# Two transformer layers on one core: the whole first-layer feed-forward is put ahead of the attention loop, and the second layer's weight transform goes one product to a gap

## The chip, the cores and the metric

The kernel runs on one core of a Trainium2 chip. The metric is device time in microseconds (us), the median of several runs. One execution was also recorded by the hardware profiler; all views of the profile below are of that one.

## The reference, cut to what matters

The input is 2 batches of 1024 tokens, 256 wide. Each of two layers normalises the tokens and adds an attention branch and a feed-forward branch, both computed from the same normalised tokens:

```
x = x + linear_attention(xn) + ffn0(xn)      # first layer, xn = layernorm(x)
x = x + softmax_attention(xn) + ffn1(xn)     # second layer, 16 heads of 16, rotary q and k
ffn0: silu(xn @ wu.T) * (xn @ wg.T) @ wd.T   # weights made ternary, 1024 hidden
ffn1: the same shape; its input and its hidden layer each go through a
      Walsh-Hadamard transform and a sign vector (SU_ug, SU_dp)
```

The kernel never transforms the tokens of ffn1. It transforms the three weight matrices once instead. A transform over 256 is a product with a 128x128 Hadamard matrix in each of two halves, and then the sum and the difference of the halves. So the effective up and gate weights are `su * (H @ w[half 0] + H @ w[half 1])` and `su * (H @ w[half 0] - H @ w[half 1])`. The down weights are handled alike over 1024, with three levels of sums and differences ("butterflies") behind the products.

## The kernel before, in words

**Two stretches.** The first layer, the second layer's attention heads of the first half of the heads of batch 0, and the search for the score maxima of the first unit stand in a prologue that a planner orders. The second layer's softmax attention is a loop written out by hand, and it takes everything else in as filler.

**The planner** (`Plan`, lines 158 to 269) records the prologue's operations in groups ("norm 1", "piece 3", "search 2" and so on), gives each a cost (`cost`, line 341), and sets them in an order by list scheduling: the operation that can begin first goes first, and between several on one engine the longest remaining chain wins. `LEADS` (line 48) holds four numbers for each group, one an engine, that are added to that chain. They do no work; they only move groups against each other. `BURST` is the planned cost of one search step.

**First-layer feed-forward.** The 2048 tokens are eight pieces of 256 columns. A piece (`ffn0`, line 750) is 8 hidden blocks of 128: 8 TensorE products each into the PSUM tile `pug` (4 for up, 4 for gate, since the tokens are split into a high and a low fp32r half `xs`), then ScalarE's tanh, two VectorE products (or, with `by_pool`, one VectorE product, a ScalarE `gate` copy and a GpSimd product), and the split of the result into `hid` high and low by ScalarE and GpSimd. Then 32 down products into `py`, and two additions to `x`. Pieces 0 to 3 are recorded wide (two blocks at a time), pieces 4 and 5 (`AHEAD = 2`, line 47) with `by_pool`, and pieces 6 and 7 (`piece0`, line 829) are filler of the loop.

**The search** (`search`, line 1294) finds the score maxima of the first unit: 32 steps, each one tile `sc` of two PSUM banks, 4 products of 32 rows (two heads by high and low), and one VectorE reduction of 128x1024 into `peak`. The step's two heads lie on two of the four 32-row groups of the array; step j+1 has the other two. There are two such two-bank tiles ("pair").

**The loop** (line 1463) has 8 units (batch, group of 4 heads). Units 0 to 6 have 32 slots each. A slot begins with a burst of 10 products on all four row groups: the scores of the next unit into `scm` (for the maxima, reduced by VectorE into `peak`) and the scores of this unit into `sce` (ScalarE's exponential into `pr`). Behind each burst comes a gap, which holds, every other iteration, 8 products with the values (`po`), the heads of the next half (`pqkv`, `pt`) in units 0, 2 and 4, and filler. `fill` (line 1339) spreads the filler by planned cost: what is left over the slots that are left. `go_on` and the marks SOON, FIRST, SECOND, BOTH decide at which point of a slot a generator goes on. Unit 7 has no `scm`; its 16 bursts are 12 products of `sce`.

**The filler in order**: pieces 6 and 7, the weight transform (`hadamards`, line 1050), the norms of the second batch, and the eight pieces of ffn1 (`ffn`, line 524: 32 fp32 products into `pug` and 16 into `py` each).

**The weight transform before.** `load_raw` (line 963) fetches six raw halves of 512 KB on SyncE's queue into a ring of three tiles that the norms and splits share. `hadamard_in` (line 976) does two products `pw` of 128x512 in one gap, and makes the sum and the difference out of PSUM: per half two ScalarE `eff` products and two VectorE `eff` operations. `hadamard_down` does the same with the down weights, one VectorE product each, and the butterflies run beside it on VectorE, GpSimd and ScalarE.

All recorded operations pass through one line of the file (316), so groups are told apart by their tiles.

Of the kernel before, what the change touches and what calls it, by code (L numbers as in the profile page):

```python
# [46 lines left out]
AHEAD = 2  # L47
LEADS = {
    "norm 0a": (-475, -452, -511, -447),
    "norm 0b": (-470, -454, -445, -428),  # L50
    "norm 1": (206, -498, -315, -178),
    "project 0": (-283, -287, -271, -286),
    "project 1": (-379, -378, -411, -385),
    "state 0": (-460, -471, -464, -465),
    "attend 0": (-328, -267, -237, -351),
    "attend 1": (-359, -315, -855, -567),
    "wuT0": (162, -329, -317, -571),
    "wgT0": (-376, -396, -368, -395),
    "wdT0": (-512, -476, -556, -527),
    "piece 0": (-333, -279, -282, -449),  # L60
    "piece 1": (-242, -206, -275, -311),
    "piece 2": (-363, -220, -404, -211),
    "piece 3": (-515, -540, -507, -534),
    "norm1 0": (-316, -213, -275, -243),
    "heads 0": (-257, -293, -242, -251),
    "norm1 1": (-308, -257, -154, -234),
    "heads 1": (-323, -80, -413, -578),
    "search 0": (-842, -831, -846, -843),
    "search 1": (-260, -228, -261, -275),
    "search 2": (-273, -536, -274, -367),  # L70
    "search 3": (-1183, -1191, -1182, -1171),
    "norm 2": (-418, -435, -436, -416),
    "norm 3": (-414, -434, -376, -387),
    "project 2": (-625, -621, -635, -600),
    "project 3": (-821, -804, -840, -810),
    "state 1": (-1258, -1149, -1268, -1233),
    "attend 2": (-298, -223, -266, -308),
    "attend 3": (-351, -334, -344, -324),
    "piece 4": (-302, -105, -189, -341),
    "piece 5": (-325, -374, -399, -449),  # L80
}
FREE = ("stats", "mv", "rstd", "shift", "rz", "part")
BURST = 0.65
# [275 lines left out]
def tile_two_layers(ctx: ExitStack, tc: tile.TileContext, a: dict, out: bass.AP):  # L359
# [469 lines left out]
    def piece0(cc):  # L829

        yield from ffn0(cc, load_raw if cc == 7 else lambda: split0(cc + 1))

# [116 lines left out]
    su_ug = load(const, "su_ug", a["su_ug"], [P, 2])  # L949
# [8 lines left out]


    raws = [("wdT1", 0), ("wdT1", 1), ("wgT1", 0), ("wgT1", 1), ("wuT1", 0), ("wuT1", 1)]  # L960
    loaded = []

    def load_raw(count=2):
        for _ in range(count):
            if raws:
                name, n = raws.pop(0)
                raw = at.tile([P, 2, C], F32, tag="stage", name="raw", bufs=3)
                if name == "wdT1":
                    view = a[name].rearrange("(k p) n -> p k n", p=P)[:, 4 * n : 4 * n + 4, :]
                    sync.dma_start(out=raw.rearrange("p a (b n) -> p (a b) n", b=2), in_=view)  # L970
                else:
                    view = a[name].rearrange("(k p) n -> p k n", p=P)[:, :, n * C : (n + 1) * C]
                    sync.dma_start(out=raw, in_=view)
                loaded.append(raw)

    def hadamard_in(name, tag):

        eff = const.tile([P, 2, E], F32, tag=tag, name=f"eff_{name}")
        had[name] = eff
        for n in range(E // C):  # L980
            cols = slice(n * C, (n + 1) * C)
            raw = loaded.pop(0)
            pw = []
            for k in range(2):
                pw.append(bank("pw"))
                mm(pw[k], [(hm, raw[:, k, :])])
                if k == 0:
                    yield C * COL
            load_raw(1)
            yield C * COL, SOON  # L990
            for m in range(2):
                scalar.mul(eff[:, m, cols], pw[1], su_ug[:, m : m + 1])
                op = ALU.subtract if m else ALU.add
                vector.scalar_tensor_tensor(eff[:, m, cols], pw[0], su_ug[:, m : m + 1], eff[:, m, cols], ALU.mult, op)
            for t in pw:
                shut(t)
            yield 0.0

    def hadamard_down():
        wd1 = const.tile([P, NB, D], F32, tag="wC", name="wd1")  # L1000
        had["wdT1"] = wd1
        there = []
        for n in range(2):
            raw = loaded.pop(0)
            for i in range(2):
                pw = bank("pw")
                mm(pw, [(hm, raw[:, i, :])])
                if i:
                    load_raw(1)
                yield C * COL, SOON  # L1010
                e = 4 * n + 2 * i
                vector.tensor_mul(
                    wd1[:, e : e + 2, :], pw.rearrange("p (k n) -> p k n", k=2), ws_dp.unsqueeze(1).to_broadcast([P, 2, D])
                )
                shut(pw)
                yield 0.0
            there.append(4 * n)
            if n == 0:
                background.append(butterflies(wd1, there))
# [29 lines left out]

    def hadamards():  # L1050
        yield from hadamard_down()
        yield from hadamard_in("wgT1", "wA")
        yield from hadamard_in("wuT1", "wB")
# [240 lines left out]
    def search(part):  # L1294

        for i in range(STEPS // 4):
            j = part // 2 * 16 + part % 2 * 2 + i // 2 * 4 + i % 2
            sc = pair("sc")
            plan.burst = True
            burst(scores_of(0, j, sc))  # L1300
            plan.burst = False
            scores_max(0, j, sc)
            yield
# [35 lines left out]
    def fill(us, queue, k=0, alone=False):  # L1339


        spent[k] = begun = max(spent[k], -1.0) - us
        while spent[k] < 0 and queue:
            when = waits.get(queue[0], 0)
            if ordered[0] and when == SOON and alone and spent[k] - begun < LEAD:
                spent[k] = min(spent[k], -LEAD)
            elif ordered[0] and (when in (FIRST, SECOND) or (when == SOON and spent[k] > -LEAD)):
                break
            step(queue, k)
        if not queue:  # L1350
            spent[k] = max(spent[k], 0.0)

    def go_on(*when):

        if filler and waits.get(filler[0], 0) in when:
            step(filler)
# [24 lines left out]
    ffn0_cost = 8 * NB * F * PASS + 2 * D * NB * 2 * PASS  # L1381
# [44 lines left out]
    for cc in range(4, 4 + AHEAD):  # L1426
# [7 lines left out]
    split0(4 + AHEAD)  # L1434
# [3 lines left out]
    layer0 = [piece0(cc) for cc in range(4 + AHEAD, 8)]  # L1438
    filler += [*layer0, hadamards(), lambda: norm1(2), lambda: norm1(3)]
    filler += [ffn1(cc) for cc in range(8)]  # L1440
    left[0] = (4 - AHEAD) * ffn0_cost + 2 * norm_cost + 12 * C * COL + 8 * ffn1_cost + 3 * heads_cost + attention_cost
# [7 lines left out]
    def slot(weight, heads=True):  # L1449
# [6 lines left out]
        fill(max(share - heads, 0.0), filler, alone=heads == 0.0)  # L1456
# [6 lines left out]
    for u in range(len(units) - 1):  # L1463
        if u in (0, 2, 4):

            if u:
                while any(g in filler for g in layer0):
                    step(filler)
# [56 lines left out]
def _layout(i):  # L1525


    def cols(v):
        return v.reshape(-1, P).T

    def halves(kind):
# [18 lines left out]
        "su_ug": cols(i["L1_ffn_SU_ug"]),  # L1550
# [23 lines left out]
```

## Time and profile before

| | us |
|---|---|
| median of 3 runs (878.51 to 878.73) | 878.65 |
| the profiled execution, device time | 879.28 |
| its span, first to last instruction | 877.5 |
| prologue, to the first `scm` product | 204.0 |
| units 0 and 1 of the loop | 89.4 and 97.4 |
| units 2 to 6, each | 83.8 to 86.2 |
| unit 7 with the end | 59.7 |

The profiled execution is 0.63 us above the median. A unit's length is the distance of its first burst from the next unit's, read off the timeline. One first-layer piece's GpSimd and ScalarE work can be read from the list of groups: `act` 750 ns and `hid` 751 ns on GpSimd, `gate` 472 ns on ScalarE, each of 128x256. In the list of groups an fp32 product shows as two records and an fp32r product as one. TensorE's durations there overlap, since products are pipelined, so this text takes distances from start to start where it wants a price.

### The profile page before, as it was taken

The numbers are of one execution on the slowest core, as the hardware profiler recorded it, in microseconds if no ns is written. First come the engines' busy times: TensorE is split into PE (matmuls) and PEld (weight loads), VectorE is DVE, ScalarE is ACT, GpSimd is POOL, SyncE is SP. The second block draws the span as 40 slices with busy tenths as digits, with TensorE's granted clock in tenths as the row PEclk, the third lists the DMA queues.
The fourth block names the chain that finished last, engine by engine and source line by source line (L and its number), as shares of the span: only waits on it lengthen the run. The fifth ranks groups of instructions, "written<-read, shape, count | busy, mean of one in ns | idle before, by whom it ended". The sixth has DMA issues, their size and how long they took to land.

```text
span 877.5 us, 14602 instructions
## 1 busy us (share of the span) xinstructions
PE 848.7 (97%) x6048; PEld 507.7 (58%) x6048; DVE 578.5 (66%) x957; ACT 446.1 (51%) x660; POOL 211.1 (24%) x285
## 2 busy tenths in 40 slices
PE   8999999999999989899999999999999999999997
PEld 5699866675556535455555555555555555555543
DVE  5887575876877778557866656577675766666311
ACT  6646465514666466345554544455454544444654
POOL 2656867522552133004400000054000000000000
PEclk9999999999999999999999999999999999999999
DMA  9200000000000200000000000000000000000001
GB/s 304 90 1 1 1 1 1 1 25 1 1 26 1 70 27 1 1 1 1 1 1 1 1 1 1 1 1 19 31 1 1 1 1 1 1 1 2 1 5 44
DMA packets 11313, 14.77 MB, mean 17 GB/s; under 512 B 1264, under 2 KB 8944, under 8 KB 11248
## 3 DMA queue, kind: packets, MB, share of 16 engines
q1 hardware_dynamic: 11248, 13.85, 4.7%
q8 instruction: 47, 0.77, 0.3%
q14 instruction: 18, 0.15, 0.1%
HBM read 11.75 MB, written 2.10 MB: 16 GB/s over the span
## 4 chain that ended last, share of the span: by engine, by line
PE 83%; DVE 10%; ACT 4%; issue 2%; DMA 1%; POOL 0%; SPq 0%; ACTq 0%; DVEq 0%; POOLq 0%
PE pug L316 18%; PE scm L316 16%; PE py L316 14%; PE po L316 13%; PE sce L316 8%; PE pqkv L316 5%; DVE peak L316 4%; PE pt L316 4%; PE pkv L316 2%; ACT pr L316 1%; PE sc L316 1%; PE pq L316 1%; DVE act L316 1%; PE pw L316 1%; DVE t_wgT L316 1%
## 5 line engine op out<-in xcount | busy, mean ns | idle before, releaser
L316 ACT ACTIVATE pr<-sce 128x1024 f32<-128x1024 f32 x256 | 260.5, 1024 | 268.6 <-PE sce L316 268.5
L316 DVE TENSOR_REDUCE peak<-scm 128x2 f32<-128x1024 f32 x224 | 274.0, 1223 | 159.9 <-PE scm L316 157.6
L316 PE MATMUL po<-pr,va 128*17 128x512 f32 x1024 | 124.9, 596 | 0.0
L316 PE MATMUL sce<-qk_hi 32*128 32x512 f32 x512 | 122.4, 496 | 2.0 <-DVE peak L316 1.1
L316 PE MATMUL scm<-qk_hi 32*128 32x512 f32 x448 | 112.1, 496 | 2.9 <-DVE peak L316 2.2
L316 PEld LDWEIGHTS scm<-qk_hi 32*128 32x128 f32 x448 | 41.5, 182 | 111.6 <-DVE peak L316 42.0
L316 PE MATMUL sce<-mx,ones_r 32*128 32x512 f32 x512 | 97.0, 392 | 0.1
L316 PE MATMUL sce<-ql,qk_hi 32*128 32x512 f32 x512 | 96.9, 393 | 0.0
L316 POOL CAST tops<-nm 128x16 fp32r<-128x16 f32 x16 | 3.6, 226 | 372.6 <-DVE nm L316 367.6
L316 PE MATMUL scm<-qk_hi,ql 32*128 32x512 f32 x448 | 89.3, 394 | 0.0
L316 PE MATMUL pug<-xnT,eff_wuT 128*128 128x256 f32 x256 | 72.4, 392 | 0.0
L316 PE MATMUL pug<-xnT,eff_wgT 128*128 128x256 f32 x256 | 69.8, 395 | 0.9 <-DVE hid L316 0.9
L316 PE MATMUL py<-wd,hid 128*128 128x256 f32 x256 | 67.1, 398 | 1.8 <-DVE xnT L316 1.8
L316 DVE SCALAR_TENSOR_TENSOR act<-act,pug 128x256 f32<-128x256 f32 (+1 forms) x112 | 50.5, 452 | 25.7 <-ACT act L316 21.0
L316 PEld LDWEIGHTS po<-pr,va 128*17 128x17 f32 x1024 | 22.8, 96 | 63.0 <-issue 61.3
L316 PEld LDWEIGHTS py<-wd,hid 128*128 128x128 f32 x256 | 45.5, 190 | 23.2 <-issue 18.7
L316 POOL TENSOR_TENSOR hid<-act,hid 128x256 fp32r<-128x256 f32 (+1 forms) x48 | 44.4, 930 | 51.6 <-ACT hid L316 39.9
L316 PEld LDWEIGHTS pug<-xnT,eff_wgT 128*128 128x128 f32 x256 | 45.0, 189 | 18.9 <-issue 13.2
L316 PEld LDWEIGHTS pug<-xnT,eff_wuT 128*128 128x128 f32 x256 | 45.6, 189 | 15.4 <-issue 10.7
L316 DVE TENSOR_TENSOR x<-py,x 128x256 f32<-128x256 f32 x68 | 27.8, 418 | 39.0 <-PE py L316 38.5
L316 PEld LDWEIGHTS sce<-mx,ones_r 32*128 32x128 f32 x512 | 46.4, 183 | 11.0 <-ACT mx L316 0.5
L316 PEld LDWEIGHTS sce<-qk_hi 32*128 32x128 f32 x512 | 45.8, 182 | 10.4 <-ACT pr L316 4.9
(146 smaller groups left out, 1338.3 us busy)
## 6 DMA issues: line engine op xcount, KB each, us to landing
out<-x SPq DMA_DIRECT2D x16, 128.0 KB, 1.7
x<-in_x SPq DMA_DIRECT2D x3, 512.0 KB, 9.4
both<-in_wuT SPq DMA_DIRECT2D x1, 1024.0 KB, 9.5
both<-in_wgT SPq DMA_DIRECT2D x1, 1024.0 KB, 10.7
wdT<-in_wdT SPq DMA_DIRECT2D x1, 1024.0 KB, 13.2
raw<-in_wdT SPq DMA_DIRECT2D x2, 512.0 KB, 3.6
raw<-in_wgT SPq DMA_DIRECT2D x2, 512.0 KB, 3.3
raw<-in_wuT SPq DMA_DIRECT2D x2, 512.0 KB, 3.4
```

The costliest lines, as they stand in the source:

```text
L316: return call(*map(real, args), **{k: real(v) for k, v in kw.items()})
```

## The change

- All of pieces 4 to 7 are recorded in the planner's prologue with `by_pool` (`AHEAD` and `piece0` go).
- A search step pair is one burst: 8 products on all four row groups into two tiles, then two reductions. `BURST` is 0.70 for the two, where it was 0.65 for one. `LEADS` has new numbers for all groups.
- `load_raw` issues three whole loads of 1 MB at the loop's start, into the tiles that held the ternary weights of the first layer (`wA`, `wB`, `wC`). In the program SyncE issues gate, up, down in this order.
- The sums and differences of the halves are made on the raw weights, ahead of the products, by GpSimd (`sums_in`): 4 differences into `less` and 4 sums in place, 128x512 each. The sign vector goes into the Hadamard matrix once (`hm_su`, two small VectorE products).
- `hadamard_in` and `hadamard_down` do one product in a gap and then move on to the next gap; the PSUM result is copied out by ScalarE or VectorE in turn, with no arithmetic. Two slots of `pause` stand ahead.
- `fill` is left out where the slot's share is used up, and a generator marked BOTH as filler goes on at any of the slot's points but LAST.

Counted in the two programs, TensorE's products are the same 4882. VectorE has 18 instructions fewer, ScalarE 12 more and GpSimd 24 more.

In the changed program unit 0's gaps hold the heads and the twelve `pw` products, each in a gap of its own or beside heads; ffn1 begins two slots before unit 1.

```diff
-AHEAD = 2
 LEADS = {
-    "norm 0a": (-475, -452, -511, -447),
+    "norm 0a": (-1158, -1159, -1192, -1189),
...
+    "piece 6": (-1028, -1111, -943, -903),
+    "piece 7": (40, -15, 116, 8),
 }
-BURST = 0.65
+BURST = 0.7
...
+    hm_su = load_row(const, "su_ug", D).rearrange("p (m n) -> p m n", m=2)
+    for m in range(2):
+        vector.tensor_mul(hm_su[:, m, :], hm_su[:, m, :], hm)
...
+    def load_raw():
+        for name, tag, n in (("wdT1", "wC", D), ("wgT1", "wA", E), ("wuT1", "wB", E)):
+            had[name] = load_w(const, name, a[name].shape[0], n, (tag, 1))
+
+    def sums_in(name, there):
+        w = had[name]
+        for n in range(0, E, C):
+            cols = slice(n, n + C)
+            less = const.tile([P, C], F32, tag="hid0", name="less", bufs=4)
+            gpsimd.tensor_tensor(less, w[:, 0, cols], w[:, 1, cols], ALU.subtract)
+            yield 0.0, BOTH
+            gpsimd.tensor_tensor(w[:, 0, cols], w[:, 0, cols], w[:, 1, cols], ALU.add)
+            there[name, n] = less
+            yield 0.0, BOTH
+
+    def next_gap():
+        yield 0.0, BOTH
+        yield 0.0
+
+    def hadamard_in(name, there):
+        w = had[name]
+        for n in range(0, E, C):
+            while (name, n) not in there:
+                yield from next_gap()
+            cols = slice(n, n + C)
+            for m, r in enumerate((w[:, 0, cols], there[name, n])):
+                pw = bank("pw")
+                mm(pw, [(hm_su[:, m, :], r)])
+                yield C * COL, SOON
+                (vector.tensor_copy if m else scalar.copy)(w[:, m, cols], pw)
+                shut(pw)
+                yield from next_gap()
...
     def search(part):
-        for i in range(STEPS // 4):
-            j = part // 2 * 16 + part % 2 * 2 + i // 2 * 4 + i % 2
-            sc = pair("sc")
+        for t in range(CT):
+            j = (part // 2 * CT + t) * 4 + part % 2 * 2
+            scs = [pair("sc") for _ in range(2)]
             plan.burst = True
-            burst(scores_of(0, j, sc))
+            burst(scores_of(0, j, scs[0]) + scores_of(0, j + 1, scs[1]))
             plan.burst = False
-            scores_max(0, j, sc)
+            for p in range(2):
+                scores_max(0, j + p, scs[p])
             yield
...
-            elif ordered[0] and (when in (FIRST, SECOND) or (when == SOON and spent[k] > -LEAD)):
+            elif ordered[0] and (when in (FIRST, SECOND, BOTH) or (when == SOON and spent[k] > -LEAD)):
...
-    for cc in range(4, 4 + AHEAD):
+    for cc in range(4, 8):
         record(f"piece {cc}", ahead0(cc, by_pool=True))
...
-    split0(4 + AHEAD)
+    load_raw()
...
-    layer0 = [piece0(cc) for cc in range(4 + AHEAD, 8)]
-    filler += [*layer0, hadamards(), lambda: norm1(2), lambda: norm1(3)]
+    filler += [pause(2), hadamards(), lambda: norm1(2), lambda: norm1(3)]
...
-        fill(max(share - heads, 0.0), filler, alone=heads == 0.0)
+        if share > heads:
+            fill(share - heads, filler, alone=heads == 0.0)
```

## The prediction

> **What bounds the kernel now.** I read the page's head and its chain first. Then I read the busy times by stretch (prologue, units of the loop), and at last the timeline of single gaps.
>
> ```profile
> span 877.5 us, 14602 instructions
> ...
> PE 848.7 (97%) x6048; PEld 507.7 (58%) x6048; DVE 578.5 (66%) x957; ACT 446.1 (51%) x660; POOL 211.1 (24%) x285
> ...
> PE 83%; DVE 10%; ACT 4%; issue 2%; DMA 1%; POOL 0%; SPq 0%; ACTq 0%; DVEq 0%; POOLq 0%
> ```
>
> TensorE is busy 97% of the span and is 83% of the chain, so a change pays only by taking time from TensorE. Moving its work is worth nothing unless it fills or opens a hole. The next view says where the holes are: columns are the stretch, its length, then busy time of TensorE, weight loads, VectorE, ScalarE and GpSimd.
>
> ```profile
> 125.00:150.00 25.00, 24.83 (x145) 17.02 (x144) 14.27 (x26) 15.63 (x37) 18.56 (x23) 1.00 0.00 1
> ...
> 204.00:293.40 89.40, 86.47 (x702) 52.66 (x700) 65.94 (x104) 52.83 (x84) 35.76 (x55) 0.98 0.04 13
> 293.40:390.80 97.40, 90.36 (x619) 46.39 (x618) 66.98 (x103) 50.25 (x69) 16.72 (x18) 0.98 0.05 17
> 390.80:476.50 85.70, 85.65 (x633) 46.87 (x632) 60.60 (x93) 43.45 (x59) 22.76 (x39) 1.00 0.00 1
> ```
>
> Unit 2 (390.8 to 476.5) has no hole; units 0 and 1, which hold the two pieces and the weight transform, have 2.9 and 7.0 us. In the prologue TensorE idles 10.3 us of the first 200, 3.5 of them in the first 25, where loads come in; GpSimd is busiest there, 18.6 of 25 us.
>
> A gap's price is read off unit 2's timeline, from one burst's first `scm` to the next.
>
> ```profile
> 455.19 0.50 PE L316 MATMUL scm<-qk_hi 32*128 32x512 f32 x2
> ...
> 456.09 1.91 PE L316 MATMUL po<-pr,va 128*17 128x512 f32 x16
> 457.93 0.50 PE L316 MATMUL scm<-qk_hi 32*128 32x512 f32 x2
> ...
> 458.83 1.13 PE L316 MATMUL py<-wd,hid 128*128 128x256 f32 x4
> 459.98 0.50 PE L316 MATMUL scm<-qk_hi 32*128 32x512 f32 x2
> ...
> 463.33 0.50 PE L316 MATMUL scm<-qk_hi 32*128 32x512 f32 x2
> ...
> 465.73 0.50 PE L316 MATMUL scm<-qk_hi 32*128 32x512 f32 x2
> ```
>
> A slot with `po` takes 2.74. From 463.33 one with three fp32 products takes 2.40; the one at 468.48, with four, takes 2.82. So a product of 256 columns costs 0.43, and the burst with its changes of shape 1.1. Two products would come to 1.96, but the slot at 457.93 takes 2.05, and so does a slot with an empty gap (204.0). That is the **floor**: the burst's two tiles come free only after VectorE's reduction (1.22 us) and the exponential. Summed by these prices, the 128 slots of units 2 to 5 come out within 1% of what was measured, so what units 0 and 1 take beyond them is stall: 15.8 us.
>
> **The change, part by part**, against the profiled execution's 879.28.
>
> 1. *Two pieces move into the prologue.* A piece has 64 + 32 fp32r products. Gaps of 12 and 20 of them take 2.53 and 3.51, so one costs 0.12; 192 cost 23.0 in either place. The loop gives them back except where a gap falls below the floor. I laid the prices on the changed program's order. In units 0 to 6, 34 gaps are short where 31 were, and lose 4.9 us where they lost 3.1. Unit 7 gets four products fewer and one more gap without filler, which I put at 0.4. Prologue +23.0, loop -23.0 + 1.8 + 0.4 = **-20.8**.
>
> 2. *The merged search.* The 32 steps took TensorE 17.6 us from start to next start, in 21 places: ten steps alone at 0.66, and eleven pairs, seven at 0.68. In the rows below, the pair at 116.34 ran four-wide in 0.68; the next could not, as its second tile was still being reduced.
>
> ```profile
> 116.34 0.51 PE L316 MATMUL sc<-qk_hi 32*128 32x512 f32 x4
> ...
> 118.83 0.50 PE L316 MATMUL sc<-qk_hi 32*128 32x512 f32 x2
> 119.17 0.40 PE L316 MATMUL sc<-qk_hi,ql 32*128 32x512 f32 x2
> 120.12 0.49 PE L316 MATMUL sc<-qk_hi 32*128 32x512 f32 x2 [0.56 <-DVE peak L316]
> ```
>
> The change makes 16 pairs: 16 x 0.68 = 10.9, **-6.8** at best. A pair needs both tiles free, so two reductions (2.45 us) must lie between bursts. In the changed order the products between two pairs cost 2.5 to 4.6 us, once 1.6. If VectorE were late at each by 120.12's 0.56, 9.0 us would be lost again, 2.2 more than is won. I take -6.8, since nearly all gaps are long enough.
>
> 3. *The transform's stalls.* Before, two `pw` in a gap held the three single banks until ScalarE and VectorE had made the sums (two 0.69 and two 0.75 us operations).
>
> ```profile
> 309.86 0.50 PE L316 MATMUL scm<-qk_hi 32*128 32x512 f32 x2
> ...
> 313.11 1.12 PE L316 MATMUL pw<-raw,hadamard 128*128 128x512 f32 x2 [1.22 <-ACT eff_wgT L316]
> 314.16 0.50 PE L316 MATMUL scm<-qk_hi 32*128 32x512 f32 x2
> ```
>
> This slot took 4.30 and its follower 4.36, while the unstalled one at 307.05 took 2.81. A third lost 0.27. One product a gap and one plain copy (0.58 to 0.68 us) leaves no such wait: **-3.3**. Bounds 0 and -3.3.
>
> 4. *The first layer's tail in unit 0.* The slots at 253.51 and 257.89 took 4.38 and 4.00 against 3.25 and 2.60 by price, where `py` waited for the last `act` and the next split. Without pieces there, **-2.5**. Bounds 0 (the heads' own `qk_hi` and `mx` copies stand in the same slot) and -2.5.
>
> 5. *GpSimd's sums.* Eight operations of 128x512, by the nearest rows 1.27 (`wd`) to 1.54 us (`had_wd`), 11 us in all. In the changed order they stand between one chunk's `rot` and its `ks`, which TensorE's transposes wait for. A chunk of heads is 2.7 us of GpSimd in two slots of 4.8. Five chunks carry sums and butterflies too, 28 us against 24 of time. So GpSimd falls up to 5 us behind, and the chain has about an iteration of slack, some 3 us. **+2.0**, the part that is not covered; bounds 0 and +5.
>
> 6. *Loads.* Three loads of 1 MB are last in SyncE's queue, with only the output stores behind. Gate and up wait for the last `pug` reader, down for the last `py`, at the loop's start. At the 304 GB/s of the page's first slice, 3 MB take 10 us. The first `pw` stands behind six slots, 15 us by price. So **0**; were that cover gone, each us late is one us of TensorE.
>
> 7. *The planner's new numbers.* No row prices an order. Before, the prologue's 204.0 held 157.6 of priced products and 17.6 of search; 28.8 was start-up, changes of shape and waits. I keep it: **0**. Bounds: -6.8, all idle time after the first 25 us, and +10.6 (second rival).
>
> 8. *Norms and butterflies in unit 1* cost 6.9 of the stalls (328.6 and 359 to 372) and are not edited: **0**. Bounds -6.9 and 0.
>
> Sum: +23.0 - 6.8 - 20.8 - 3.3 - 2.5 + 2.0 = -8.4. 879.28 - 8.4 = 870.9 in the profiled execution, and less its 0.63 above the median **870.3 us**.
>
> [...] TensorE's granted clock (the figure behind the busy times) fell to half twice.
>
> ```profile
> 204.00:206.00 2.00, 1.27 (x12) 0.49 (x10) 1.47 (x2) 1.22 (x2) 0.59 (x3) 1.00 0.00 0
> ...
> 208.00:209.00 1.00, 1.00 (x3) 0.56 (x2) 0.22 (x1) 0.48 (x1) 0.00 (x0) 0.50 0.00 0
> ```
>
> From 207.3 and from 367.7 it stood at 0.5 for 3.4 us, which cost 1.7 us each, in step 8's stalls and at the loop's start. Ahead of the first TensorE was idle only in pieces under 0.8 us. I keep both (**0**); a third, as the changed order has one more empty gap near the start, would be +1.7. [...]
>
> **The rivals.**
>
> *It gains more* (about 860): the prologue's holes close (-6.8) and unit 1's stalls shrink, since ffn1 begins earlier and the norms meet fewer queued operations (half of -6.9). 870.3 - 6.8 - 3.5 = 860. For it: nothing in the counts stands against it. Against: the norms' code is the same, and the prologue's waits are many and small, the longest 1.6 us.
>
> *The merge isn't worth its wait* (about 876): the tile pairs wait for two reductions at most bursts, so step 2 gives nothing or little: 870.3 + 6.8 = 877.1, 876 with part of it. For it: four of eleven adjacent pairs stalled before. Against: the products now planned between pairs.
>
> *Slower: GpSimd becomes the prologue's bound* (about 882). Two `by_pool` pieces add 16 x (0.75 + 0.75) + 2 x 1.29 = 26.6 us of GpSimd to a stretch that grows by 16.2. From 50 to 175 it was busy 83.6 of 125 us (67%); it would be 110 of 141 (78%). Its chain feeds TensorE's `py`, which already waited for `hid` at 117.8 (0.42). If the prologue can grow only as GpSimd's work does, it grows by 26.6 and not 16.2: +10.4, so 880.7, and with step 5's upper end (+3 more) 883. It decides once GpSimd leaves TensorE over 9 us of waits more. Against: 78% is not full, and the four engines are planned together.
>
> **How the numbers follow.** Forecast (864 to 875): 0.60. More gain (below 864): 0.14. Merge without worth (875 to 879): 0.12. GpSimd (above 879): 0.14. The range 861 to 880 leaves out about a tenth below and a tenth above. Two tenths of a per cent, 1.8 us, is about what a measurement of this kernel can tell from no change. Below 876.9: 0.60 + 0.14 + half of the third case = 0.80. Between: the other half and a little of the last, 0.08. Above 880.4: 0.12.
>
> **What would show it.** The first `scm` at about 220 us (step 1, 2, 7): at 226 or later with TensorE waiting for GpSimd's `hid`, the third rival; with `sc` waiting for `peak`, the second. Units 0 and 1 together at about 176 us against 186.8, units 2 to 6 at 80 to 84 each, unit 7 at about 58. `pw` without a wait for ScalarE (step 3). `pt` waiting for GpSimd's `ks` in slots 10 to 18 would be step 5. If units 2 to 6 don't get shorter, the pricing of gaps is wrong altogether.

## The result, and the profile after

The changed kernel takes **887.75 us** (median of 4 runs, 884.06 to 891.01) against 878.69 beside it: ratio 1.0100, 95% interval 1.0058 to 1.0143. Run again beside other experiments (e6) it took 884.80 (883.53 to 885.66), ratio 1.0074, interval 1.0057 to 1.0091. It is slower, by 0.6 to 1.4%, where I had forecast 870.3 and a range to 880. The profiled execution took 886.54 us.

The head of the page and its chain of waits, after:

```profile
span 884.6 us, 14626 instructions
...
PE 847.1 (96%) x6048; PEld 506.5 (57%) x6048; DVE 578.4 (65%) x939; ACT 450.3 (51%) x672; POOL 233.1 (26%) x309
...
PE 77%; DVE 12%; ACT 5%; issue 3%; POOL 2%; DMA 1%; SPq 0%; ACTq 0%; POOLq 0%; DVEq 0%
```

TensorE's own work is the same (it even reads 1.6 us less), but its share of the chain fell from 83 to 77%, while VectorE's rose from 10 to 12 and GpSimd's from 0 to 2%. So TensorE waits more, and not for one engine: its listed waits add up to 18.5 us for VectorE (16.0 before), 8.7 for ScalarE (5.5) and 5.3 for GpSimd (2.4). The stretches say where. Columns are as in the prediction: stretch, length, TensorE, weight loads, VectorE, ScalarE, GpSimd, granted clock. First after (75 us of start-up, the rest of the prologue, units 0, 1 and 2), then the prologue before:

```profile
0.00:75.00 75.00, 64.29 (x349) 48.30 (x349) 58.28 (x135) 40.31 (x74) 31.78 (x32) 0.95 0.36 117
75.00:230.05 155.05, 149.43 (x1024) 119.69 (x1024) 107.15 (x216) 83.14 (x186) 103.97 (x127) 1.00 0.03 12
230.05:318.92 88.87, 81.27 (x557) 38.07 (x556) 66.53 (x96) 46.40 (x66) 41.87 (x53) 0.98 0.05 18
318.92:409.95 91.03, 87.39 (x631) 49.78 (x631) 58.52 (x87) 44.25 (x58) 7.99 (x11) 0.98 0.00 1
409.95:493.90 83.95, 83.76 (x627) 45.45 (x626) 59.40 (x90) 43.24 (x58) 22.34 (x38) 1.00 0.00 1
```

```profile
0.00:75.00 75.00, 69.31 (x405) 54.42 (x406) 56.41 (x146) 44.19 (x81) 37.05 (x37) 1.00 0.35 116
75.00:204.03 129.03, 124.41 (x778) 91.97 (x776) 94.10 (x183) 59.63 (x129) 73.83 (x88) 1.00 0.02 5
```

| us | before | forecast | after |
|---|---|---|---|
| prologue, to the first `scm` | 204.0 | 220.2 | 230.05 |
| TensorE idle in the first 75 us | 5.7 | 5.7 | 10.7 |
| units 0 and 1 | 186.8 | 176 | 179.9 |
| units 2 to 6 | 427.1 | 400 to 420 | 416.0 |
| unit 7 to the end | 59.7 | about 58 | 58.6 |
| units 2 to 7 together | 486.7 | 472.9 (what the sum leaves) | 474.6 |

The loop got shorter as planned, but for 3.9 us in units 0 and 1. The prologue grew by 26.0 us and not by 16.2. Of its 6.0 us of new idle time 5.0 lie in the first 75 us, where the moved pieces have not begun. The waits of TensorE there (what waits, what it waits for; sum, times, longest) are:

```profile
PE pt L317 <- ACT xn L317: 2.6, 2, 1.5
PE pq L317 <- DVE kc L317: 2.5, 1, 2.5
PE pa L317 <- DVE kv L317: 1.8, 1, 1.8
PE warm L317 <- POOL ident masks.py:199: 1.5, 1, 1.5
PE pa L317 <- DVE rz L317: 1.3, 1, 1.3
```

Before, the longest of these but `warm` was this one:

```profile
PE pa L316 <- DVE kv L316: 1.0, 1, 1.0
```

And the clock behind the longest wait, by stretches of 2 us:

```profile
36.00:38.00 2.00, 0.85 (x2) 0.49 (x3) 2.00 (x7) 0.83 (x2) 0.27 (x1) 1.00 0.00 0
39.00:41.00 2.00, 2.00 (x9) 1.58 (x8) 2.00 (x7) 1.26 (x2) 0.00 (x0) 0.50 0.00 0
```

TensorE waits until 37.15, and from 38.5 for 3.41 us it has half the clock. There are four such stretches in this execution (11.2, 38.5, 233.1 and 325.2 us), two of them in the prologue, where the kernel before had none after its start. By the granted 0.50, 3.41 us of products cost 1.7 us more, an estimate from the clock alone (in e6 two stretches less went with 3.0 us less).

### The profile page after: what moved, and what is told of

It is laid out like the page before. It is cut to its first block, busy times and chain, and to the rows that moved or that the text cites. A ratio compares the mean times of both kernels' runs of the same rounds, so it can differ in the third digit from the quotient of the medians.

```text
span 884.6 us, 14626 instructions
## 1 busy us (share of the span) xinstructions
PE 847.1 (96%) x6048; PEld 506.5 (57%) x6048; DVE 578.4 (65%) x939; ACT 450.3 (51%) x672; POOL 233.1 (26%) x309
## 4 chain that ended last, share of the span: by engine, by line
PE 77%; DVE 12%; ACT 5%; issue 3%; POOL 2%; DMA 1%; SPq 0%; ACTq 0%; POOLq 0%; DVEq 0%
PE pug L317 16%; PE scm L317 15%; PE po L317 12%; PE py L317 12%; PE sce L317 8%; PE pqkv L317 4%; PE pt L317 4%; DVE peak L317 4%; PE pkv L317 2%; DVE act L317 1%; ACT pr L317 1%; PE pq L317 1%; PE sc L317 1%; ACT act L317 1%; POOL hid L317 1%
## 5 line engine op out<-in xcount | busy, mean ns | idle before, releaser
L317 PE MATMUL pug<-xnT,wgT 128*128 128x256 f32 x256 | 71.3, 402 | 1.9 <-ACT xnT L317 1.0
L317 PE MATMUL pug<-xnT,wuT 128*128 128x256 f32 x256 | 72.2, 394 | 0.0
L317 PE MATMUL py<-wdT,hid 128*128 128x256 f32 x256 | 67.3, 396 | 0.0
L317 PEld LDWEIGHTS pug<-xnT,wgT 128*128 128x128 f32 x256 | 44.8, 190 | 22.3 <-issue 15.0
L317 PEld LDWEIGHTS py<-wdT,hid 128*128 128x128 f32 x256 | 44.9, 190 | 21.2 <-issue 17.0
L317 PEld LDWEIGHTS pug<-xnT,wuT 128*128 128x128 f32 x256 | 46.2, 191 | 14.9 <-issue 10.0
```

The costliest lines, as they stand in the source:

```text
L317: return call(*map(real, args), **{k: real(v) for k, v in kw.items()})
```

## The experiments

My first theory was **A**: the new planner numbers order the first 75 us badly. Its rivals: the two pieces' GpSimd work (G, my third rival), and a merge that gives little (M).

### e2: the merged search alone

```diff
 (the kernel before)
-BURST = 0.65
+BURST = 0.7
     def search(part):
...
+            scs = [pair("sc") for _ in range(2)]
+            burst(scores_of(0, j, scs[0]) + scores_of(0, j + 1, scs[1]))
```

> The kernel before with the merged search alone (and its planned cost of 0.70): old planner numbers, pieces 6 and 7 and the old transform in the loop. Theory A (the loss of 10 us in the prologue comes from the new order of its first 75 us, the merge itself is worth what was forecast): the first scm product comes at 197 to 200 us against 204.0, the total falls by 4 to 7 us, and no sc product waits over 0.3 us for peak. Rival M (the merge gives little, since other things than the search's own time bound the prologue): first scm at 202 to 205, total within 2 us of the kernel before.

Measured 879.08 against 879.71: ratio 0.9990 (0.9976 to 1.0004), no difference. First `scm` at 201.74. The search took TensorE 12.7 us instead of 17.6, but the rest of the prologue, with the same products, grew by 2.7. So in the old order M is nearly right: half of TensorE's saved time turned into waiting. Of the 2.3 us by which the first `scm` came earlier, this execution lost 1.8 again in unit 0, where the half clock lasted from 203.5 to 210.3 us, 6.8 us, and 3.4 in the kernel before.

### e4: the two pieces back in the loop, the new order kept

```diff
 (the changed kernel)
-    for cc in range(4, 8):
+    for cc in range(4, 6):
         record(f"piece {cc}", ahead0(cc, by_pool=True))
...
+    layer0 = [piece0(cc) for cc in range(6, 8)]
-    filler += [pause(2), hadamards(), ...
+    filler += [*layer0, pause(2), hadamards(), ...
```

> The changed kernel with pieces 6 and 7 back in the loop as filler ahead of the transform; the merged search, the new planner numbers and the new transform stay. The planned order of all four engines is that of the changed kernel up to about 148 us. Theory A (the new order of the first 75 us costs about 10 us): the loss stays, first scm at 207 us or later (204.0 - 6.8 + 9.8), total 878 to 884. Rival G (the two pieces' GpSimd work makes the loss, through hid): first scm at 197 to 200, TensorE idle in the first 75 us as in the kernel before (5.7 us), total 868 to 874.

Measured 896.64, ratio 1.0184 (1.0161 to 1.0208), the slowest of all and far above what A expected. First `scm` at 215.25. Its prologue holds the same work as that of e2 (and the two small `su_ug` products), in the other order. The stretches of e4, then of e2:

```profile
0.00:75.00 75.00, 62.81 (x351) 48.53 (x352) 58.35 (x135) 40.71 (x76) 33.01 (x33) 0.98 0.36 117
75.00:150.00 75.00, 71.80 (x475) 60.13 (x474) 41.22 (x96) 44.25 (x97) 57.34 (x65) 1.00 0.00 1
150.00:215.25 65.25, 57.68 (x356) 37.28 (x356) 55.59 (x98) 18.39 (x40) 21.09 (x29) 0.96 0.00 1
```

```profile
0.00:75.00 75.00, 68.69 (x402) 53.80 (x403) 56.08 (x145) 44.19 (x81) 37.01 (x37) 1.00 0.34 116
75.00:150.00 75.00, 72.22 (x461) 55.78 (x459) 49.33 (x103) 39.60 (x86) 54.84 (x63) 1.00 0.00 1
150.00:201.74 51.74, 47.88 (x321) 34.29 (x322) 43.10 (x82) 20.76 (x45) 18.90 (x25) 1.00 0.03 11
```

TensorE idles 12.2 us of the first 75 in e4 and 6.3 in e2. The early loss is there without the pieces: G falls for it, A stands for these 5.9 us. But the prologue is 13.5 us longer than that of e2, and the rest is of another kind. From 150 us on e4 idles 7.6 us, and most of that is the wait of my second rival:

```profile
PE sc L317 <- DVE peak L317: 4.7, 7, 1.1
```

Behind it, from 210.1, TensorE had half the clock for 13.65 us, over the first `scm`. In the whole profile e4 has 27.3 us of half clock, the changed kernel 13.7. So e4's total and the end of its prologue don't price the early order. The changed kernel has the two pieces to put between the search's bursts; there no `sc` waits for `peak`, and it idles 1.9 us from 150 us on.

### e5: the two sign products out of the prologue

What in the order is bad? On VectorE two `su_ug` products, which the change adds and which I had left out of my sum, took 0.8 us each right ahead of the late `kc`.

```diff
 (the changed kernel)
     hm_su = load_row(const, "su_ug", D).rearrange("p (m n) -> p m n", m=2)
-    for m in range(2):
-        vector.tensor_mul(hm_su[:, m, :], hm_su[:, m, :], hm)
...
     load_raw()
+    for m in range(2):
+        vector.tensor_mul(hm_su[:, m, :], hm_su[:, m, :], hm)
```

> The changed kernel with the two VectorE products that put the sign vector into the Hadamard matrix (128x128, 0.81 us each at 35.06 us in the trace, ahead of a kc addition for which TensorE then waits 2.5 us at 34.7) taken out of the prologue and issued at the loop's start. Nothing else is edited; the planner's order changes only where it had them. Theory A1 (these two products are part of the loss, with the half-clock window of 3.4 us that follows the wait): first scm 2.5 to 4.4 us earlier than 230.05, total 2.5 to 4.4 us below the changed kernel's 887.75. Rival (the place is taken by the next wait, VectorE being late there anyway): first scm within 1 us of 230, total within 1 us.

Measured 885.67, ratio 1.0061 (1.0043 to 1.0079), within the changed kernel's own spread. First `scm` at 229.92, and `pq` still waits 2.4 us for `kc`: the rival. (The products may have cost about 1 us all the same: this profile has 10.2 us of half clock in its prologue, and e3 and e9, which have as much there and the changed kernel's prologue, reach the first `scm` at 231.22 and 230.84.) In their place a `ws_ug` product of 128x8 now took 1.11 us, of a kind that takes 0.17 in the kernel before. So it is not what stands there, but how long anything lasts there.

### e10: GpSimd's additions beside it made short

The rows of VectorE and GpSimd in the changed kernel:

```profile
31.74 2.19 DVE L317 SCALAR_TENSOR_TENSOR t_wgT<-both,sc_wgT,t_wgT 128x1024 fp32r<-128x1024 f32 x1
33.85 1.30 DVE L317 TENSOR_SCALAR ws_ug<-ws_ug 128x8 f32<-128x8 f32 x2
35.06 1.55 DVE L317 TENSOR_TENSOR su_ug<-su_ug,hadamard 128x128 f32<-128x128 f32 x2
...
36.69 0.74 DVE L317 TENSOR_TENSOR kc<-pkv,kvb 128x256 f32<-128x256 f32 x2
```

```profile
31.58 4.68 POOL L317 TENSOR_TENSOR x<-x,ob 128x512 f32<-128x512 f32 x3
```

Three GpSimd additions run from 31.6 to 36.3, and until they end VectorE's `t_wgT`, `ws_ug` and `su_ug` take 2.19, 1.30 and 1.55 us; the next `t_wgT`, at 37.36 with no addition beside it, takes 1.27. The experiment cuts them, and a fourth at 23.8, to 8 of 256 columns; so it leaves out most of the output bias of the first batch.

```diff
 (the changed kernel)
+            n = 8 if c < 2 else D
-            gpsimd.tensor_tensor(x2, x2, ob.unsqueeze(1).to_broadcast([P, 2, D]), ALU.add)
+            gpsimd.tensor_tensor(x2[:, :, 0:n], x2[:, :, 0:n], ob[:, 0:n].unsqueeze(1).to_broadcast([P, 2, n]), ALU.add)
+            plan.ops[-1].cost = 2 * D / 472 + 0.19
```

> The changed kernel with the four GpSimd additions of the attention's output bias for the first batch (x<-x,ob, 128x512, three of them in a row from 31.6 to 36.3 us) cut to 8 of 256 columns; the bias of the other columns is left out for that batch. Their planned cost is kept, so the planned order of all engines is that of the changed kernel, operation by operation. Theory P (VectorE operations with inputs in SBUF last until the GpSimd operation beside them ends: two ws_ug products of 128x8 take 1.30 us there and 0.23 in the kernel before, t_wgT 2.2 against 1.3; so kc is late and TensorE waits 2.5 us at 34.7, and the half clock follows): the wait of pq for kc falls from 2.5 to under 1 us, ws_ug to about 0.2, the half-clock window at 38 goes, first scm 2.5 to 5 us earlier than 230.05. Rival (those stretches are VectorE's own, or TensorE waits for the next operation in the queue anyway): the wait stays over 1.5 us, first scm within 1 us of 230.

```profile
29.69 1.32 DVE L317 SCALAR_TENSOR_TENSOR t_wgT<-both,sc_wgT,t_wgT 128x1024 fp32r<-128x1024 f32 x1
30.93 0.25 DVE L317 TENSOR_SCALAR ws_ug<-ws_ug 128x8 f32<-128x8 f32 x2
31.10 0.48 DVE L317 TENSOR_TENSOR su_ug<-su_ug,hadamard 128x128 f32<-128x128 f32 x2
...
31.66 0.74 DVE L317 TENSOR_TENSOR kc<-pkv,kvb 128x256 f32<-128x256 f32 x2
```

Same order, same VectorE operations: 2.19 became 1.32, 1.30 became 0.25, 1.55 became 0.48. From `t_wgT` to `kc` they took 1.97 us instead of 4.95, so `kc` gained 3.0 us here; it came 5.0 earlier, and the other 2.0 lie ahead of these rows, where the fourth addition was short too and this execution had no half clock at 11.2. The wait of `pq` was gone and with it the half clock behind it (one stretch, at 48.9, remains in the prologue). First `scm` at 224.74, total 882.80, ratio 1.0042 (1.0028 to 1.0055). Theory P holds. These rows don't show by what the two engines hold each other up.

The kernel before has the same additions, and there too VectorE takes longer beside them (and beside a GpSimd product just ahead of them):

```profile
29.23 3.38 DVE L316 TENSOR_SCALAR t_wgT<-both,sc_wgT 128x1024 fp32r<-128x1024 f32 x2
33.04 1.78 DVE L316 SCALAR_TENSOR_TENSOR t_wgT<-both,sc_wgT,t_wgT 128x1024 fp32r<-128x1024 f32 x1
```

In the changed kernel the first of these took 1.42 us, and the second takes 1.27 where no addition runs beside it. But in the old order no product waited for `kc`. So the additions are not new; what is new is that TensorE's next input stands behind them. The additions were not cut in the kernel before, so what that would be worth there is not shown.

### e11: idle products where TensorE waits

Are the half-clock stretches a thing of their own, or the waits' doing? In the other runs' profiles the first of them in a row follows a 3.41 us stretch in which TensorE had idled 1.2 us (e7, ahead of 11.0) to 2.7 us (e8, ahead of 286.5); at the loop's start 0.8 was enough (233.1 in the changed kernel, 207.3 in the kernel before).

```diff
 (the changed kernel)
+COVER = {(28, 0): 4, (17, 0): 3, (78, 0): 10, (116, 1): 7, (128, 0): 5}
         for op in order:
+            for k, call in enumerate(op.calls):
+                for _ in range(COVER.get((op.i, k), 0)):
+                    self.cover()
...
+    plan.cover = lambda: emit(nc.tensor.matmul, (po[:, 0:P],), dict(lhsT=ident, rhs=ident, start=True, stop=True))
...
+                for _ in range(3 if u + i == 0 else 0):
+                    plan.cover()
```

> The changed kernel with 32 idle products of 128x128 (identity by identity, into a bank of PSUM that the loop overwrites before it is used) put on TensorE just ahead of the products that wait longest: 4 and 3 before the first two pt, 10 before the pq that waits 2.5 us for kc, 7 and 5 before the two pa that wait 1.8 and 1.3 us, and 3 in the empty first gap of the loop. Nothing waits less for it. Theory C (TensorE's clock falls to half for 3.41 us behind a window in which it idled over 1.3 us): no half-clock window in the prologue, where the two profiles of the changed kernel have two and one; first scm 1 to 3.5 us earlier than 228.5 to 230.0, the runs spread less than 884 to 891, total 881 to 884. Rival (the half clock comes on its own, or the idle products delay the real ones): windows remain, total 885 to 890.

The covered kernel's first 75 us:

```profile
0.00:75.00 75.00, 69.08 (x415) 55.07 (x416) 58.76 (x135) 41.54 (x77) 33.24 (x33) 1.00 0.34 117
```

In its profile there is no half clock from 6.4 to 880.2 us, in the loop neither. Total **882.49** (10 runs, 881.92 to 884.42), ratio 1.0040 (1.0028 to 1.0053): TensorE does more and the kernel is faster. Theory C holds. In the prologue the gain was 1.6 us (first `scm` 228.43 against 230.05) and not 3.4; against e6, which had one stretch there, it was nothing. Why a stretch costs less than its 1.7 us is not shown; a wait behind a slow stretch may get shorter by itself. The eight runs of the uncovered kernel go with their mean clock: 883.5 and 884.1 at 0.996, 884.1 at 0.994, 885.6, 885.7 and 886.5 at 0.992, 889.0 and 891.0 at 0.988. So their spread goes with the number of such stretches. The kernel before ran at 0.992 to 1.000, on average some two stretches fewer (one lowers the mean by 0.0019).

### e6: the changed kernel again

> The changed kernel itself once more, as the reference for the runs beside it and to see how its runs spread. Theory C (the spread of 884 to 891 us comes from a differing number of half-clock windows of 3.41 us, each about 1.7 us, which follow a window in which TensorE was idle for 1.3 us or more): the profiled run's mean clock and time go together, 1.7 us for each window; first scm at 229 to 232. Rival: the times spread at one and the same number of such windows.

First `scm` at 228.46, two half-clock stretches (52.1 and 321.8) where the first profile had four, 883.53 us where that had 886.54: 3.0 less for two stretches less, 1.5 each.

### e8: the old transform in the changed kernel

```diff
 (the changed kernel, with load_raw, hadamard_in, hadamard_down of the kernel before)
-    filler += [pause(2), hadamards(), ...
+    filler += [pause(4), hadamards(), ...
```

> The changed kernel with the weight transform of the kernel before (half loads of 512 KB into the shared ring, two pw in a gap, sums and differences made out of PSUM by ScalarE and VectorE, signs as a factor there; four slots of pause ahead for the loads). All pieces stay ahead of the loop, the search stays merged. Step 3 of the forecast (two pw in a gap stall TensorE by 3.3 us, GpSimd's sums cost 2.0): units 0 and 1 together 1 to 4 us longer than the 179.9 of the changed kernel. Rival V (in unit 0 of the changed kernel VectorE's work ahead of the peak reductions has taken the place of those stalls, 5.2 us of scm waiting for peak; one product a gap gains nothing): units 0 and 1 at 177 to 181.

Measured 889.57, ratio 1.0125 (1.0107 to 1.0142). Units 0 and 1 took 182.2 against 179.9 and 178.3 in the two profiles of the changed kernel, with one half-clock stretch in them against two and one. The largest wait in them is the one that step 3 was about, a `pw` for which no single bank is free (here until VectorE has read the `pt` of `att`):

```profile
286.16 1.72 PE L317 MATMUL pw<-raw,hadamard 128*128 128x512 f32 x2 [2.72 <-DVE att L317]
```

A half-clock stretch follows at 286.5. So beside the heads the new transform is worth 3.9 us at the same number of half-clock stretches, GpSimd's sums already paid: step 3 stands in its sign. (Before the change the transform stood in unit 1, without heads beside it.)

### e3: the sums on VectorE

```diff
 (the changed kernel)
-            gpsimd.tensor_tensor(less, w[:, 0, cols], w[:, 1, cols], ALU.subtract)
+            vector.tensor_tensor(less, w[:, 0, cols], w[:, 1, cols], ALU.subtract)
...
-            gpsimd.tensor_tensor(w[:, 0, cols], w[:, 0, cols], w[:, 1, cols], ALU.add)
+            vector.tensor_tensor(w[:, 0, cols], w[:, 0, cols], w[:, 1, cols], ALU.add)
```

> The changed kernel with its eight sums and differences (less and the sums in place) on VectorE and not on GpSimd. Theory S (a VectorE operation with two SBUF inputs lasts as long as the GpSimd sum beside it, and ks queues behind the sums): in unit 0 rot and had_wd take 0.4 to 0.8 us and not 1.1 to 1.5, the waits of TensorE for ks (1.39) and for peak (1.29) in slots 12 and 15 go, and unit 0 is 2 to 3 us shorter than 88.9; the prologue stays at 230. Rival (VectorE gets 8 operations of about 0.6 us more, 5 us, in front of the reductions that free the burst's tiles): unit 0 the same or up to 3 us longer.

Measured 888.49, ratio 1.0093 (1.0076 to 1.0111): no gain. The wait for `ks` (1.4 us) went, and `rot` took 0.43 us at most instead of 1.24, but TensorE waited 8.0 us for `peak` in unit 0 instead of 5.2. The sums are no better on the engine that the burst's tiles depend on.

### e9: the copies of `pw` on ScalarE

```diff
 (the changed kernel)
-                (vector.tensor_copy if m else scalar.copy)(w[:, m, cols], pw)
+                scalar.copy(w[:, m, cols], pw)
```

> The changed kernel with all eight copies of pw out of PSUM on ScalarE; in the changed kernel every second one (four of 0.68 us) is on VectorE. Theory V (in unit 0 TensorE waits 5.2 us for VectorE's peak reduction, which stands in VectorE's queue behind ql, rot, had_wd and the pw copies): the waits of scm for peak in unit 0 fall by 1 to 2.5 us, unit 0 is that much shorter than 87.3 to 88.9. Rival (the copies aren't what stands ahead of the late reductions, or ScalarE's exponentials become late in turn): unit 0 the same within 0.5 us, or sce waits for pr.

Measured 886.47, ratio 1.0068 (1.0039 to 1.0097). The waits for `peak` in unit 0 fell from 5.2 to 4.6, unit 0 is 88.3: the rival. One slot's 0.6 us went; the copies aren't what makes `peak` late.

### e13: no butterflies

What unit 0 still waits for, after:

```profile
PE scm L317 <- DVE peak L317: 5.2, 6, 1.3
PE pt L317 <- POOL ks L317: 1.4, 1, 1.4
PE sce L317 <- ACT pr L317: 0.5, 1, 0.5
```

and one of these slots, from its burst at 281.31 on VectorE's queue:

```profile
281.77 0.42 DVE L317 TENSOR_TENSOR ql<-pt,qk_hi 128x256 fp32r<-128x256 f32 x1 [1.09 <-ACT qk_hi L317]
282.11 0.68 DVE L317 TENSOR_TENSOR wdT<-pw,ws_dp 128x512 f32<-128x512 f32 x1
282.70 0.42 DVE L317 TENSOR_TENSOR rot<-qk,qs 128x256 f32<-128x256 f32 x1
283.04 1.22 DVE L317 TENSOR_REDUCE peak<-scm 128x2 f32<-128x1024 f32 x1
...
284.31 0.50 PE L317 MATMUL scm<-qk_hi 32*128 32x512 f32 x2 [0.97 <-DVE peak L317]
```

The heads' `ql` and `rot` and the transform's `wdT` stand ahead of the reduction that frees the tile; the burst is 0.97 late.

```diff
 (the kernel of e11)
-        background.append(butterflies(wd1, there))
...
-            vector.tensor_mul(
-                wd1[:, e : e + 2, :], pw.rearrange("p (k n) -> p k n", k=2), ws_dp.unsqueeze(1).to_broadcast([P, 2, D])
-            )
+            scalar.copy(wd1[:, e : e + 2, :], pw.rearrange("p (k n) -> p k n", k=2))
```

> The kernel with the idle products (882.49 us, no half-clock window) without the down weights' butterflies, and with its four pw products copied by ScalarE and not scaled by VectorE: the butterflies and that scaling are left out. GpSimd's sums for gate and up, the heads and TensorE's products stay. Theory V2 (what unit 0 loses is the transform's work on VectorE and GpSimd between the heads' rot and the peak reductions; by the prices of the gaps slots 12, 15, 18 and 23 take 1.34, 1.65, 0.94 and 0.92 us more than their products): those four fall to under 0.4 each, unit 0 is 3 to 5 us shorter than 87.3, units 0 and 1 end at 173 to 176 against 177.7. Rival (the heads' own chain and the gaps without filler are the limit, whatever the transform does): unit 0 at 86 to 87.5.

This kernel leaves out the butterflies and a scaling of the down weights. Unit 0 took 82.24 instead of 87.26 (e11), total 877.75, ratio 0.9987 (0.9976 to 0.9999). Its waits in unit 0:

```profile
PE scm L320 <- DVE peak L320: 1.9, 3, 1.1
```

The four slots fell from 1.34, 1.65, 0.94 and 0.92 us over their price to under 0.15, 0.19, 0.35 and under 0.15. V2 holds: in unit 0, beside the heads, the down weights' part of the transform costs 5.0 us.

### e7 and e12: a version that is faster than both

If the order decides, the merge needs numbers of its own. All groups' numbers were chosen anew for e2; the loop and the rest are the kernel before.

```diff
 (the kernel of e2)
-    "norm 0a": (-475, -452, -511, -447),
...
-    "piece 5": (-325, -374, -399, -449),
+    "piece 5": (-1840, -2180, -2860, -2145),
```

> The kernel before with the merged search and BURST 0.70, as in the merge-only run, but with planner numbers of its own for all groups (the planned prologue is 187.5 us long against 193.9 of the merge-only run). Pieces 6 and 7 and the old transform stay in the loop. Theory A2 (the merge's 5 to 6 us on TensorE are real and are lost to waits only where the order wasn't made for it): first scm at 195 to 198 us against 201.7, search 11 to 12 us of TensorE, total 872 to 876. Rival M (VectorE's and GpSimd's chains bound the prologue whatever the order): first scm 201 to 204, total 877 to 880.

**874.05**, ratio 0.9945 (0.9929 to 0.9962). The first `scm` came only at 200.8, but two half-clock stretches (11.0 and 48.5) lie ahead of it, where e2 had none until the loop's start and two there. So the same idle products were put into e7:

```diff
 (the kernel of e7, with the lines of e11)
+COVER = {(58, 0): 4, (104, 0): 2, (114, 0): 9}
```

> The retuned merge-only kernel (874.05 us) with 18 such idle products: 4 before the pkv that waits 1.1 us for xnT, 2 before the pk that waits 0.6 for kc, 9 before the pa that waits 2.3 us, 3 in the loop's first gap. Theory C: its two half-clock windows of the prologue (11.0 and 48.5 us) go, first scm 2 to 3.5 us earlier than 200.8, total 870 to 872.5. Rival (the half clock comes on its own): windows remain, total 873 to 876.

```profile
span 869.3 us, 14673 instructions
...
PE 843.0 (97%) x6084; PEld 507.6 (58%) x6084; DVE 577.9 (66%) x957; ACT 446.4 (51%) x660; POOL 210.7 (24%) x285
```

**871.44** (871.00 to 875.31), ratio 0.9922 (0.9897 to 0.9946): the fastest of all. First `scm` at 198.93, no half clock in the profile, though two of its runs show 0.995 and 0.997. Of the change it holds the merged search alone; the pieces and the transform are where they were before. How much of it is the merge and how much the new numbers isn't shown: the kernel before was not run with numbers of its own chosen anew, and neither was the changed kernel.

## Why the prediction was wrong, by its steps

The miss is 15.6 us in the profiled execution (886.54 against 870.9): 9.9 in the prologue, 3.9 in units 0 and 1, 1.7 in the rest of the loop, and the rest around it.

1. *Two pieces move.* Right in the loop: units 2 to 7 came out at 474.6 against the 472.9 that the sum leaves for them. In the prologue their products cost what they should.
2. *The merged search.* Its own term is right: in the changed kernel the 16 pairs took 11.2 us (16 x 0.67 and a few late), 6.4 less than 17.6, and none waited for `peak`. But that this shortens the prologue doesn't follow from it, as e2 shows (-2.3). Time taken from TensorE is worth nothing where the next product isn't ready. And in the new order the products between the pairs, on which I rested it, come in part from the moved pieces: without two of them `sc` waited 4.7 us for `peak` (e4).
3. *The transform's stalls.* Right in sign; steps 3 and 5 together were put at -1.3, and by e8 the new transform gains 3.9 in its new place.
4. *The first layer's tail in unit 0.* Those waits are gone, but I didn't ask what takes their place in the same slots.
5. *GpSimd's sums, +2.0.* The mechanism is there (`less` ran in front of `ks`, TensorE waited 1.4 us), and so about the size. A second one I hadn't seen: beside a sum, VectorE's `rot` lasts 1.24 us instead of 0.42, and the reduction behind it is late.

```profile
251.40 1.27 POOL L317 TENSOR_TENSOR less<-wgT 128x512 f32<-128x512 f32 x1
...
251.71 1.24 DVE L317 TENSOR_TENSOR rot<-qk,qs 128x256 f32<-128x256 f32 x1
252.87 1.21 DVE L317 TENSOR_REDUCE peak<-scm 128x2 f32<-128x1024 f32 x1
```

6. *Loads, 0.* Right: no `pw` waits for one in the changed kernel.
7. ***The planner's new numbers, 0: the step that failed.*** The prologue's idle time rose from 10.3 to 16.3 us, 5.0 of it in the first 75, and two half-clock stretches came with it. In this profile 23.0 for the pieces, less 6.4, plus 6.0 idle and 3.4 of half clock make the 26.0. The parts are good to a microsecond or two: 1.5 of the old idle time lay in the search's 17.6 and is counted twice, and e11 found only 1.6 of the 3.4 to be had back. I kept the old idle time because no row prices an order; but the order of the changed program was there to be read, operation by operation, and the places where VectorE's long operations now ran beside GpSimd's in front of TensorE's next input could have been found in it. e4 shows the loss without the pieces, e10 one of its causes, worth 3.7 us against e6, which has one half-clock stretch in its prologue like e10 (5.3 against the first profile, which has two). What the rest is made of (`xn` in the first norm 2.6, `kv` and `rz` 3.1, `hid` 2.4 against 0.4) was not taken apart.
8. *Norms and butterflies, 0.* Wrong by its place: the butterflies weren't edited, but they moved from unit 1's gaps to unit 0, beside the heads, and cost 5.0 there (e13).

*The clock.* I kept two half-clock stretches and put a third at 1.7. The profile had four. What brings them on no run shows in full; e11, with idle products in the waits and a clock of 1.00, bears it out that idle time has a part in it, and 1.2 to 2.7 us of it in 3.41 were enough.

*The rivals.* The one on the other side named the right sign and nearly the right first `scm` ("226 or later"), but for another reason: `hid` made TensorE wait 2.0 us more, not 9. GpSimd did slow the prologue, through VectorE and not as the bound. That the merge isn't worth its wait was nearly true of the merge alone, but not through `peak`, for which `sc` waited 1.0 us in e2 and 1.5 before; in e4 it waited 4.7.

## What to carry to other kernels

Work taken off a busy engine pays only where its next input is ready: before you sum savings, read in the changed order what each engine's queue holds ahead of the next input of the bound engine, new small operations included. Operations of VectorE and GpSimd on SBUF side by side can take nearly as long as one after the other, as they did here: VectorE's 2.05 us of e10 and GpSimd's three additions (1.27 us each at 26.6 us in the kernel before) took 5.0 together. Not every pair did (below), so a pair is to be priced from rows of its own. Waits of one or two microseconds on TensorE can cost twice, by themselves and by the clock behind them (2.5 us for `kc` and then 3.41 us at 0.50 in the changed kernel). A few idle products in such waits cost nothing here and took the half clock out: with 32 of them e11 took 882.49 us, against 887.75 and 884.80 without.

## What the runs showed of the hardware

- In the changed kernel a VectorE operation of 128x8 (`ws_ug`) took 0.15 us alone, at 36.54, and up to 1.23 us beside GpSimd additions of 128x512 (three of them 4.68 us there); one of 128x256 with both inputs in SBUF (`rot`) 0.42, at 282.70, and 1.24, at 251.71. `qk`, of the same size with one input in PSUM, took 0.41 us in the middle of a GpSimd operation of 128x512 (at 271.40 in the changed kernel, GpSimd's from 271.22 to 272.50). `stats` of 128x256, also from SBUF, took 0.39 to 0.43 us each of 32 times in either kernel, the four at 27.42 in the kernel before among them, beside two GpSimd additions (26.61 to 29.15).
- The half clock came in stretches of 3.41 us or multiples of it (6.8 in e2, 13.65 in e4), and within an execution they began on a grid of 3.41 us: 11.2, 38.5, 233.1 and 325.2 in the changed kernel lie 8, 57 and 27 steps apart. It came after stretches of that length with TensorE idle for 1.2 (e7) to 2.7 us (e8), at the loop's start after 0.8, and not after the two with 1.6 and 1.5 us from 48.8 to 55.6 in the changed kernel's first profile, so idle time alone doesn't tell when it comes. Where the stretches begin against the kernel's work differs between executions: the waits of `pa` at 48 to 55 us fell into those two; in e6, the same program, 2.0 us of them fell into one, and the half clock followed at 52.1.
